# Layer 3's weights of eight steps queued on VectorE behind a block's joining

## Chip, cores and metric

The kernel runs on one core of one Trainium2 chip. The metric is the device time of one execution in microseconds (us); several executions are taken and their median is given. Beside them one execution was recorded by the profiler; all views of a profile in this text are of that one execution.

## The reference

Four graph layers follow one another on a matrix x of 3327 rows and 256 columns, with one adjacency matrix of 3327 x 3327 of which about one entry in a hundred is set. After each layer the input is added and the rows are normalised.

```python
x = _layernorm(x + _L0_gnn_ref(x, adj, L0_gnn_Wq, L0_gnn_Wk))
x = _layernorm(x + _L1_gnn_ref(x, adj, L1_gnn_W, L1_gnn_a))
x = _layernorm(x + _L2_gnn_ref(x, adj, L2_gnn_Wq, L2_gnn_bq, ...))
x = _layernorm(x + _L3_gnn_ref(x, adj, L3_gnn_W0, L3_gnn_W1, ...))
```

The change touches the last one, which is three graph attention layers behind one product with `W0`:

```python
def _gat_layer(h, adj, W, a):
    Wh = h @ W
    f1 = Wh @ a[:F_out]
    f2 = Wh @ a[F_out:]
    e = jax.nn.leaky_relu(f1 + f2.T, ALPHA)
    att = jnp.where(adj > 0, e, NEG_INF)
    att = jax.nn.softmax(att, axis=1)
    h_prime = att @ Wh
    return jax.nn.elu(h_prime)
h = input @ W0
h = _gat_layer(h, adj, W1, a1)
h = _gat_layer(h, adj, W2, a2)
h = _gat_layer(h, adj, W3, a3)
```

So each of the three makes a matrix of 3327 x 3327 weights, one for every pair of rows, sets those without an edge to nothing, multiplies the matrix with 256 columns and divides each row by its sum of weights.

## The kernel before

**Tiling and stages.** The rows are padded to 3328, 26 tiles of 128 (`NT`). The rows for which results are made are taken in 7 blocks (`NB`) of 512, the last of 256. A list of steps runs over the layers "0", "1", "2", "3a", "3b", "3c", in each over the blocks b, and in each block over the 26 tiles j of the rows that are summed over. Layer 3's three attentions are the last three entries (`deep(L)` is true for them). A loop over all steps (from L1552) traces the work of each step. All engines run at once, each through a queue of its own in a fixed order; only the first steps of the whole program have an order written out by hand. The order of the rest is found when the program is built, by a scheduler that takes what is ready by a priority and by estimated times. An edge between two instructions of one engine that carries no data binds the scheduler: the second is queued behind the first.

**Weights.** `Gat.weights` makes the weights of one step, 128 x 512: ScalarE writes `re` (L787), VectorE adds and multiplies with the mask into `ft` (L800). Blocks 0 to 5 of layer 3 use Strassen's seven products in place of eight. For these, sums and differences of quarters of the weights are needed: four instructions `qsum` for four steps together (`quad_sums`, L871 to L874), or four shorter `ssum` for two steps (L883 to L886). The other factor's sums, `tsums`, were written to memory in the layer before and are loaded again for each pair of steps, into three buffers, by SyncE's queue (L857).

`make_to(n)` (called at L1581) traces the weights of all steps below n that were not traced yet. In layer 3 it runs 7 steps ahead of the step whose products come next, so at a block's start the first weights of this block have been traced already, behind those of the block before.

**Products.** Each second step, `products` (L935) issues 14 matmuls of TensorE into four banks of PSUM, `po`. TensorE takes an fp32 matmul as two rows in the profile. 13 pairs make a block: 364 rows. PSUM has five banks for `po`.

**A block's end.** `finish` is a generator that `advance()` drives, one part behind each following step's products. It starts with `joined` (L943 to L980): it adds Strassen's products from the four banks into one tile, `p`. ScalarE copies one quarter (L961), and then 12 instructions of VectorE follow (L967 to L979); the last of them, L979, adds the last bank's part. The row sums are inverted (L1182, L1183), and then comes, for the 512 rows,

1. `normed` on ScalarE, four instructions that divide by the row sums (L1175 or L1177, in place on `p`),
2. `turn`: two copies of ScalarE that lay out the halves of the numbers as `planes` (L990), a transpose by DMA that SyncE's queue issues (L993, `turned<-planes`), and two copies by VectorE into `pT` (L1000),
3. `projected`: eight matmuls of TensorE with the next attention's W (`pproj<-w,pT`, L1230),
4. elu on ScalarE and VectorE (L1239, L1242, L1254), the scores of the next attention (L719), its sums (L1084, L844 to L852).

VectorE's queue holds, in the stretch from L967 to the copies L1000, both the joining and weights of the next steps. Which stands where is the scheduler's choice.

Of the kernel before, what the change touches and what calls it, by code (L numbers as in the profile page):

```python
# [33 lines left out]
def gnn_stack(ctx: ExitStack, tc: tile.TileContext, a: dict, N: int, out: bass.AP):  # L34
# [8 lines left out]
    nc = tc.nc  # L43
# [6 lines left out]
    def bw(b):  # L50
        return min(CH, NP - b * CH)
# [652 lines left out]
    class Gat:  # L704
        def __init__(self, key):
            self.last = key == "3c"
            self.quads = ("3a", "3b", "3c").index(key) + 1 if key != "1" else 0
            self.k = w.get("k_" + key)
            self.row = w["row_" + key]
            self.sd = cols.tile([P, 2, NT], F32, tag="sd", name="sd")  # L710
            self.th = cols.tile([P, NT], F32, tag="th", name="th")
            self.rh = cols.tile([P, NT], F32, tag="rh", name="rh")
            self.nrh = cols.tile([P, NT], F32, tag="nrh", name="nrh")
            self.u = {}
# [100 lines left out]
    def strassen(L, b):  # L815
        if L.key == "0":
            return 0 < b < NB - 1
        if deep(L):
            return b < NB - 1
        return L.key == "2"  # L820

    def deep(L):
        return L.i > 2
# [65 lines left out]
    def places(pos, b):  # L889


        o = H + 1
        m = {
            1: ((0, 0, o), (0, o, o)),
            2: ((0, 2 * o, o), (2, 0, o)),
            5: ((2, o, o), (2, 2 * o, o)),
            3: ((3, 0, H), (3, H, H)),
            4: ((3, D, H), (3, D + H, H)),
            6: ((1, 0, H), (1, H, H)),
            7: ((1, D, H), (1, D + H, H)),  # L900
        }
        return {
            k: [(g, pos[g][:, c : c + n]) for g, c, n in v[: bw(b) // D]]
            for k, v in m.items()
        }
# [37 lines left out]
    def joined(pos, b, c):  # L943

        w_ = places(pos, b)
        q = bw(b) // D
        o = H + 1

        def both(k):

            bank_, at, n = {
                1: (0, 0, o), 5: (2, o, o), 3: (3, 0, H), 4: (3, D, H), 6: (1, 0, H), 7: (1, D, H)
            }[k]
            v = pos[bank_][:, at : at + 2 * n].rearrange("p (s n) -> p s n", n=n)
            return v[:, :q, :H]

        c11, c12 = c[:, :q, H:], c[:, :q, :H]
        c21, c22 = c[:, q : 2 * q, H:], c[:, q : 2 * q, :H]
        add, sub = ALU.add, ALU.subtract
        z = cols.tile([P, 4], F32, tag="zc", name="zs")  # L960
        nc.scalar.copy(c22, both(1))  # L961

        def sums(k):
            v = pos[{1: 0, 5: 2}[k]][:, {1: 0, 5: o}[k] :]
            return v[:, : 2 * o].rearrange("p (s n) -> p s n", n=o)[:, :q, H]

        nc.vector.tensor_copy(z[:, :q], sums(1))  # L967
        nc.vector.tensor_copy(z[:, q : 2 * q], sums(5))
        for i in range(q):
            nc.vector.tensor_tensor(  # L970
                z[:, i : i + 1], z[:, i : i + 1], w_[2][i][1][:, H:], add
            )
            nc.vector.tensor_tensor(c[:, i, H:], c22[:, i], w_[2][i][1][:, :H], add)
        nc.vector.tensor_tensor(c22, c22, both(6), add)
        nc.vector.tensor_tensor(c21, c22, both(7), add)  # L975
        nc.vector.tensor_tensor(c12, c22, both(5), add)
        nc.vector.tensor_tensor(c22, c21, both(5), add)
        nc.vector.tensor_tensor(c21, c21, both(4), sub)
        nc.vector.tensor_tensor(c12, c12, both(3), add)  # L979
        return z[:, : 2 * q]  # L980


    def turn(x4, n, out, steps=3):
# [109 lines left out]
    def finish(L, b, pos):  # L1093
# [25 lines left out]
        if L.key == "0":  # L1119
            am = anyadj.pop(b)[:, :n]  # L1120

            if strassen(L, b):
                y4 = work.tile([P, 4, D], F32, tag="x4k", name="y4", bufs=2)
                z_ = joined(pos, b, y4)
                nc.vector.tensor_scalar(z_, z_, TINY, None, ALU.max)
            else:
                z_ = cols.tile([P, 4], F32, tag="zc", name="zc")
                for k in range(n):
                    nc.vector.tensor_scalar(
                        z_[:, k : k + 1], pos[k][:, D : D + 1], TINY, None, ALU.max  # L1130
                    )
# [38 lines left out]
        else:  # L1170

            def normed(out, src, r):

                if L.key in ("3b", "3c"):
                    nc.scalar.activation(out, src, AF.Identity, bias=less, scale=r)  # L1175
                else:
                    nc.scalar.mul(out, src, r)  # L1177

            p4 = work.tile([P, 4, D], F32, tag="stage", name="p4", bufs=4)
            if strassen(L, b):  # L1180
                z = joined(pos, b, p4)
                nc.vector.tensor_scalar(z, z, TINY, None, ALU.max)  # L1182
                nc.vector.reciprocal(z, z)  # L1183
                for k in range(n):
                    normed(p4[:, k, :], p4[:, k, :], z[:, k : k + 1])
            else:
                for k, t in enumerate(ts_):
                    ri = cols.tile([P, 1], F32, tag="ri", name="ri", bufs=4)
                    nc.vector.tensor_scalar(
                        ri, pos[k][:, D : D + 1], TINY, None, ALU.max  # L1190
                    )
                    nc.vector.reciprocal(ri, ri)
                    normed(p4[:, k, :], pos[k][:, :D], ri)
# [77 lines left out]
        if not L.hidden:  # L1271
# [10 lines left out]
            for k, t in enumerate(ts_):  # L1282
# [8 lines left out]
                if L.key == "3c":  # L1291
                    q = LASTP if t == NT - 1 else P
# [147 lines left out]
    class Layer:  # L1440
        def __init__(self, i, key, gat=False, hidden=False):
            self.i, self.key, self.is_gat, self.hidden = i, key, gat, hidden
            self.w = key
            self.gat = self.gat_next = self.sum = None
            self.late = []

    layers = [
        Layer(0, "0"),
# [28 lines left out]
    def make(s):  # L1477
        if s >= len(steps):
            return
        L, b, j = steps[s]  # L1480
        make_weights(L, b, j)
        if j % 2 and by_pairs(L, b, (j + 1) // 2):
            pairs[b, j + 1] = pair_weights(b, (j + 1) // 2)
            next(pairs[b, j + 1])
# [58 lines left out]
    extra = 0  # L1543
    ends = deque()

    def make_to(n):
        nonlocal upto
        while upto < n:
            make(upto)
            upto += 1  # L1550

    for s, (L, b, j) in enumerate(steps):  # L1552
# [6 lines left out]
        if j == 0:  # L1559
            wo, no = (CH, 4) if strassen(L, b) else (D + 1, len(tiles_of(b)))  # L1560
            pos = [
                ps_o.tile([P, wo], F32, tag="po", name="po") for _ in range(3 if end else no)
            ]
# [9 lines left out]
        ahead_of = s + LA + 1  # L1573
        if deep(L):
            ahead_of += 4 if b else min(4, j // 3)
            if b == 0 and pending:
                ahead_of = max(s + LA + 1, min(ahead_of, L.i * NB * NT + NT - 2))
            if not last:
                end_of = (L.i + 1) * NB * NT
                ahead_of = max(s + LA + 1, min(ahead_of, end_of))  # L1580
        make_to(ahead_of + extra)  # L1581
        if first:
            if j < 2:
                next(q1)
# [114 lines left out]
        if j == NT - 1:  # L1699
            if b == 0 and not last:  # L1700
                nl = layers[L.i + 1]
                L.sum = Sum()
                if nl.is_gat:
                    if nl.key == "1":
                        while "row_1" not in w:
                            next(setup)
                    nl.gat = Gat(nl.key)
                    L.gat_next = nl.gat
            if end:
                pending.append(finish_last(pos[1:], xm, 1))  # L1710
            else:
                pending.append(finish(L, b, pos))
            advance()
# [65 lines left out]
```

## Time and profile before

| | us |
|---|---|
| three runs | 2303.7, 2296.58, 2299.3 |
| median | 2299.3 |
| the profiled execution | 2297.41 |
| its span | 2295.6 |
| mean granted TensorE clock | 0.996 of full speed |
| layer 3's first block end (start of the joining) | 1419.8 |

The span runs from the first to the last instruction; the 1.8 us beside it are the start and the end of the execution. Layer 3's attention fills the last 38% of the span. Its stretches, from the windows of the trace (length, then busy time of TensorE, its weight loads, VectorE, ScalarE and GpSimd with the number of instructions, the granted clock, the share of the DMA engines, GB/s):

```
1420.00:1700.00 280.00, 272.38 (x2202) 263.25 (x2202) 261.96 (x632) 168.35 (x284) 6.14 (x13) 1.00 0.45 130
1700.00:1980.00 280.00, 272.86 (x2210) 264.27 (x2209) 260.56 (x619) 162.52 (x267) 3.38 (x14) 0.99 0.47 132
1980.00:2296.00 316.00, 299.18 (x2477) 291.65 (x2475) 293.39 (x721) 176.00 (x274) 0.10 (x1) 0.98 0.45 129
```

A line of a timeline has the start, the duration, the engine, the line of the kernel, the operation, output and input tiles and shapes, how many equal ones follow each other, and in brackets the idle time of the engine before it and what ended it. A line of the list of waits has who waited for whom, the time in all, how many times, and the longest. An instruction of VectorE can start up to about 0.1 us before the one ahead of it has ended, so costs in a row of instructions are read from start to start. PE is TensorE, PEld its weight loads, DVE is VectorE, ACT ScalarE, POOL GpSimd, SP SyncE.

### The profile page before, as it was taken

How to read it: one execution, taken by the hardware profiler on the slowest of the kernel's cores; microseconds unless marked ns; L12 is line 12 of the kernel's file. 1: busy time of each engine (PE TensorE's matmuls, PEld its weight loads, DVE VectorE, ACT ScalarE, POOL GpSimd, SP SyncE). 2: the span in 40 equal slices, each digit the busy share in tenths (PEclk: the TensorE clock that was granted, in tenths of full speed). 3: DMA queues.
4: the chain of work that ended last, by engine and by line, in shares of the span. 5: the costliest groups of instructions: out<-in, count | busy, mean ns of one | idle time of the engine just before them, and what ended most of it. 6: DMA issues, size and time to landing. Idle time of an engine off the chain costs nothing. (4 is left out here: it accounts for less than half of the span.)

```text
span 2295.6 us, 41529 instructions
## 1 busy us (share of the span) xinstructions
PE 2257.2 (98%) x15183; PEld 2004.7 (87%) x15183; DVE 1998.3 (87%) x5437; ACT 1210.3 (53%) x1982; POOL 49.4 (2%) x196
## 2 busy tenths in 40 slices
PE   9999999999999999999999999999999999999997
PEld 7788888888888877888888899999999999999997
DVE  7789999866777777898898889999899999899996
ACT  4667777764555423223223246555666555655653
POOL 0000001000000000000000000000000000000000
PEclk9999999999999999999999999999999999999999
DMA  8655565523222322132132254444444445355542
GB/s 281 192 178 179 186 195 187 161 84 89 78 72 55 105 61 81 56 100 81 56 99 71 74 171 130 133 136 143 124 129 137 131 134 148 98 152 169 149 122 58
DMA packets 186207, 286.13 MB, mean 125 GB/s; under 512 B 80413, under 2 KB 105492, under 8 KB 181396
## 3 DMA queue, kind: packets, MB, share of 16 engines
q1 hardware_dynamic: 185732, 283.22, 41.2%
q8 instruction: 120, 1.97, 0.4%
q14 instruction: 83, 0.68, 0.1%
q10 hardware_dynamic: 272, 0.26, 0.0%
HBM read 228.21 MB, written 38.44 MB: 116 GB/s over the span
## 5 line engine op out<-in xcount | busy, mean ns | idle before, releaser
L787 ACT ACTIVATE re<-u,nrh,th 128x512 f32<-128x512 f32 (+1 forms) x728 | 539.8, 778 | 343.0 <-DVE ft L800 179.7
L1644 PE MATMUL po<-v,e 128*128 128x257 f32 x1872 | 422.3, 381 | 0.9 <-ACT p L1177 0.8
L1644 PEld LDWEIGHTS po<-v,e 128*128 128x128 f32 x1872 | 352.6, 190 | 60.9 <-issue 9.8
L935 PE MATMUL po<-tsums,qsum 128*128 128x128 f32 (+1 forms) x2520 | 352.8, 275 | 1.4 <-DMA tsums<-t3b_d 0.7
L800 DVE SCALAR_TENSOR_TENSOR ft<-re,rh,mask 128x512 f32<-128x512 f32 x468 | 341.1, 747 | 2.6 <-ACT re L787 2.6
L935 PEld LDWEIGHTS po<-tsums,qsum 128*128 128x128 f32 x2520 | 316.2, 192 | 3.5 <-DVE qsum L873 1.6
L935 PE MATMUL po<-tsums,ssum 128*128 128x128 f32 (+1 forms) x2082 | 293.2, 276 | 4.0 <-DMA tsums<-t3a_d 1.7
L935 PE MATMUL po<-v,ft 128*128 128x129 f32 x1872 | 286.1, 276 | 1.3 <-DVE p L975 0.6
L935 PEld LDWEIGHTS po<-tsums,ssum 128*128 128x128 f32 x2082 | 262.6, 192 | 7.0 <-DVE ssum L885 2.0
L935 PEld LDWEIGHTS po<-v,ft 128*128 128x128 f32 x1872 | 248.2, 192 | 4.0 <-issue 1.8
L935 PEld LDWEIGHTS po<-v,e 128*128 128x128 f32 x1196 | 172.3, 191 | 37.6 <-issue 24.9
L935 PE MATMUL po<-v,e 128*128 128x129 f32 x1196 | 185.1, 275 | 0.0
L800 DVE SCALAR_TENSOR_TENSOR e<-re,rh,mask 128x512 f32<-128x512 f32 (+1 forms) x234 | 149.1, 657 | 38.4 <-PE po L1644 28.4
L524 ACT ACTIVATE ex<-ps,rq 128x512 f32<-128x512 f32 (+1 forms) x183 | 118.9, 652 | 114.7 <-PE ps L511 109.9
L511 PE MATMUL ps<-ft 128*128 128x512 f32 (+1 forms) x364 | 166.9, 564 | 0.0
L496 DVE SCALAR_TENSOR_TENSOR e<-ex,mask 128x512 f32<-128x512 f32 (+1 forms) x182 | 115.8, 650 | 49.0 <-ACT ex L694 27.1
L935 PE MATMUL po<-tsums,ft 128*128 128x128 f32 x936 | 144.2, 275 | 0.0
L525 DVE SCALAR_TENSOR_TENSOR e<-ex,mask 128x512 f32<-128x512 f32 (+1 forms) x183 | 116.8, 644 | 31.1 <-ACT ex L524 30.5
L686 PE MATMUL ps<-gT,ft 128*128 128x512 f32 (+1 forms) x336 | 129.8, 527 | 0.0
L935 PE MATMUL po<-v,qsum 128*128 128x128 f32 x840 | 128.8, 275 | 0.0
L935 PEld LDWEIGHTS po<-tsums,ft 128*128 128x128 f32 x936 | 124.9, 193 | 0.3
L660 ACT ACTIVATE ex<-ex,off 128x512 f32<-128x512 f32 x98 | 67.0, 716 | 101.7 <-DVE ex L676 69.1
(346 smaller groups left out, 3572.8 us busy)
## 6 DMA issues: line engine op xcount, KB each, us to landing
mask<-mask_d SPq DMA_DIRECT2D x30, 1664.0 KB
stage<-in_adj_a SPq DMA_DIRECT2D x78, 512.0 KB
tsums<-t_d SPq DMA_DIRECT2D x152, 256.5 KB
tsums<-t3a_d SPq DMA_DIRECT2D x77, 256.5 KB
tsums<-t3b_d SPq DMA_DIRECT2D x77, 256.5 KB
tsums<-t3c_d SPq DMA_DIRECT2D x77, 256.5 KB
mask_d<-mask SPq DMA_DIRECT2D x6, 1664.0 KB
u<-s_d SPq DMA_DIRECT2D x24, 256.0 KB
```

What stands on the lines that cost most here:

```text
L496: nc.vector.scalar_tensor_tensor(e[:, :wd], t_[:, :wd], 0.0, mask(b, j), ALU.add, ALU.mult)
L511: nc.tensor.matmul(ps[:, :wd], FT[j // 4][:, 0, (j % 4) * P : (j % 4 + 1) * P], FT[b][:, 1, :wd], start=True, stop=True,)
L524: nc.scalar.activation(t_[:, c], ps[:, c], AF.Exp, scale=rq[:, j : j + 1])
L525: nc.vector.scalar_tensor_tensor(e[:, c], t_[:, c], 0.0, mask(b, j)[:, c], ALU.add, ALU.mult)
L660: nc.scalar.activation(x[k], x[k], AF.Exp, bias=off, scale=1.0 / D**0.5)
L686: nc.tensor.matmul(ps[:, :wd], FT[j // 4][:, h, (j % 4) * P : (j % 4 + 1) * P], g[:, h, :wd], start=(h == 0), stop=(h == 1),)
L787: nc.scalar.activation(t_[:, :wd], self.u[b][:, :wd], AF.Relu, bias=self.nrh[:, j : j + 1], scale=self.th[:, j : j + 1],)
L800: nc.vector.scalar_tensor_tensor(e[:, :wd], t_[:, :wd], self.rh[:, j : j + 1], mask(b, j), ALU.add, ALU.mult,)
L935: nc.tensor.matmul(o, x, y, start=(p == 0 and g not in banks[:i]), stop=(p == NT // 2 - 1 and g not in banks[i + 1 :]),)
L1644: nc.tensor.matmul(pos[k], e[:, k * P : (k + 1) * P], V[L.i % 2][i], start=(i == 0), stop=(i == NT - 1),)
```

## The change

`joined` returns its last instruction (L979) too. For layer 3's blocks it is kept in the layer's `joined`, which is empty until the first block's end. In the first eight steps of each block for which there is one, `make_to` runs inside `issue_after`: each VectorE instruction that is traced in it gets an edge without data to the kept L979, so it is queued behind it. What is computed, the tiles and the other engines' instructions stay as they are; the scheduler orders all engines anew with the edges. The edges exist for blocks 1 to 6 of each of the three attentions, 18 block ends. `extra`, `LA` and the steps ahead are the same.

```diff
@@ joined @@
-        nc.vector.tensor_tensor(c12, c12, both(3), add)
-        return z[:, : 2 * q]
+        return z[:, : 2 * q], nc.vector.tensor_tensor(c12, c12, both(3), add)
@@ finish, layer "0" @@
-                z_ = joined(pos, b, y4)
+                z_, _ = joined(pos, b, y4)
@@ finish, other layers @@
-                z = joined(pos, b, p4)
+                z, L.joined = joined(pos, b, p4)
@@ class Layer @@
             self.late = []
+            self.joined = None
@@ the loop over the steps @@
-        make_to(ahead_of + extra)
+        if deep(L) and L.joined is not None and j < 8:
+            with tc.issue_after(L.joined.ins):
+                make_to(ahead_of + extra)
+        else:
+            make_to(ahead_of + extra)
```

## Prediction

> **What bounds the kernel now.** First the page's busy times and its chain, to see which engine sets the end:
>
> ```profile
> PE 2257.2 (98%) x15183; PEld 2004.7 (87%) x15183; DVE 1998.3 (87%) x5437; ACT 1210.3 (53%) x1982; POOL 49.4 (2%) x196
> ...
> PE 9%; DVE 4%; DMA 2%; ACT 1%; issue 1%; POOL 0%; DVEq 0%; ACTq 0%; POOLq 0%
> PE po L935 7%; DMA turned<-planes 1%; PE pproj L1230 1%; DVE ft L800 1%; ACT planes L990 1%; PE po L1644 1%; PE po L1610 0%; DVE v L800 0%; ACT re L787 0%; ACT p L1175 0%; DMA tsums<-t3c_d 0%; DVE qsum L872 0%; DVE qsum L874 0%; DVE pT L1000 0%; DVE qsum L873 0%
> ```
>
> TensorE is busy all the time and VectorE nearly. The chain runs through `turned<-planes`, `planes` and `pproj`, the path behind a block's end. So the question is what TensorE waits for, in the list of its waits and then where VectorE stands meanwhile:
>
> ```profile
> PE pproj L1230 <- DVE pT L1000: 13.3, 14, 2.3
> PE po L935 <- DMA tsums<-t3a_d: 1.7, 2, 1.4
> ...
> PE po L935 <- DVE p L975: 0.6, 2, 0.3
> ```
>
> The copies of the turned rows are by far the largest thing that TensorE waits for; 12.7 of the 13.3 us lie behind 1420 us, in layer 3, which alone the change touches. Next, VectorE's timeline at the block end of 1767 us (3b; columns: start, us, instruction):
>
> ```profile
> 1767.23 0.16 DVE L967 COPY zs<-po 128x2 f32<-128x2 f32 x1
> 1767.30 0.75 DVE L800 SCALAR_TENSOR_TENSOR ft<-re,rh,mask 128x512 f32<-128x512 f32 x1
> ...
> 1768.62 0.75 DVE L800 SCALAR_TENSOR_TENSOR ft<-re,rh,mask 128x512 f32<-128x512 f32 x1
> ...
> 1769.70 0.67 DVE L871 TENSOR_TENSOR qsum<-ft 128x512 f32<-128x512 f32 x1
> ...
> 1770.94 0.69 DVE L872 TENSOR_TENSOR qsum<-ft 128x512 f32<-128x512 f32 x1
> ...
> 1771.87 0.69 DVE L873 TENSOR_TENSOR qsum<-qsum,ft 128x512 f32<-128x512 f32 x1
> ...
> 1772.80 0.42 DVE L979 TENSOR_TENSOR p<-p,po 128x256 f32<-128x256 f32 x1
> 1773.13 0.69 DVE L874 TENSOR_TENSOR qsum<-ft,qsum 128x512 f32<-128x512 f32 x1
> ```
>
> Five weight instructions stand between the joining's first (L967) and last (L979). Behind it, on ScalarE four `normed` (2.08 us) and two `planes` (1.97 us), then SyncE's transpose, then the copy. At the end of 1812 us the same path, as VectorE's and TensorE's timelines show it:
>
> ```profile
> 1826.77 0.69 DVE L872 TENSOR_TENSOR qsum<-ft 128x512 f32<-128x512 f32 x1
> 1829.84 1.37 DVE L1000 COPY pT<-turned 128x1024 uint16<-128x1024 uint16 x2 [2.38 <-issue]
> ```
> ```profile
> 1831.27 4.54 PE L1230 MATMUL pproj<-w_l_w,pT 128*128 128x256 f32 x12 [2.23 <-DVE pT L1000]
> ```
>
> VectorE stands 2.38 us at the copy, TensorE 2.23 us for the copy. The transpose is late, so the path sets both engines; neither is at its own bound here. The granted clock in the windows behind this gap and the like one at 1879 us (last columns: clock, DMA share, GB/s):
>
> ```profile
> 1831.40:1834.90 3.50, 3.50 (x9) 2.79 (x10) 3.28 (x6) 1.36 (x3) 0.00 (x0) 0.51 0.00 0
> ...
> 1879.20:1882.70 3.50, 3.19 (x8) 2.57 (x9) 2.48 (x6) 1.08 (x3) 0.00 (x0) 0.51 0.00 0
> ```
>
> **The change, part by part.** Nothing is removed or added: returning L979's instruction and keeping it in `L.joined` issues nothing, and the edge is an order within VectorE's queue. So the instruction counts and the work stay, and the cost of the edit is in what moves. It acts at 18 block ends (3 sublayers, blocks 1 to 6); the other layers keep their order.
>
> *What leaves the joining.* One `ft` costs 0.66 us from start to start (1767.30 to 1767.96), one `qsum` 0.60 us (1770.94 to 1771.54). Two and three make 2 x 0.66 + 3 x 0.60 = 3.1 us at this end; two and two make 2.5 us in 3a; where six stand there, some 3.8 us. The queues of the changed program say the same: at 17 of the 18 ends these four to six stand right behind L979, and between L979 and the copy there are 14 or 15 VectorE instructions as before.
>
> *What comes earlier.* L979, `normed`, `planes` and the transpose come 2.5 to 3.8 us earlier. The transpose is now issued ahead of one `tsums` load that it followed. SyncE's timeline before:
>
> ```profile
> 1777.96 2.99 SPq L993 DMA_TRANSPOSE turned<-planes  x1
> 1781.05 0.53 SPq L857 DMA_DIRECT2D tsums<-t3b_d  x1
> ```
>
> The transpose's row is 2.99 us and the load starts at 1781.05, behind it. Now the transpose can start at about 1774.9 (behind the previous load of 1774.46), and be through at 1777.9; so the load, too, goes earlier. Cost nil; if the cover were gone, it is the 1.4 us of the worst wait for `tsums`.
>
> *What it brings to TensorE.* Its `pproj` stands 2 to 10 matmuls earlier in its queue (two rows of 0.112 us each: 0.4 to 2.2 us), and the copy comes 2.5 to 3.9 us earlier. The margin is 0.5 to 1.8 us, so the gaps should close. The gaps ahead of the first `pproj`, end by end from the trace: 3a 0.93, 0.39, 2.09, 1.72, 0, 0.48 = 5.6 us; 3b 0.02, 0.23, 2.23, 2.30, 0.66, 0.42 = 5.9 us; 3c 0, 0.41, 0.29, 0.55, 0.03 = 1.3 us, and 0.97 at the last end, where the queue moves the other way (10 matmuls later) and which I put at nothing. Two stretches of half clock of 3.4 us cost 1.7 us each and hang on the gaps of 2.23 and 2.30 us; the gap of 2.09 us at 1529 brought none.
>
> [...]
>
> *What VectorE allows.* From 1784 to 1832 us it is busy 45.5 of 48.0 us; its idle time is the 2.38 us at the copy. So a block can shrink by about this much, not by TensorE's 2.23 + 1.7. I take for those two ends VectorE's idle, 2.4 and 2.6 us: 3b then gives 0.25 + 5.0 + 1.1 = 6.3 us.
>
> *What comes later.* The moved weights come 0.7 to 2.1 us later. Queued behind them on VectorE is the weight work of the next steps, and TensorE's products wait for that. Measured from a weight's end on VectorE to its first use on TensorE, the lead at the ends is 0.7 to 1.8 us in 3a, 1.9 to 2.4 us at the first ends of 3b and 3c, 3 to 10 us after. Placed in the new order, all leads stay above 0.7 us, as the whole joining, 5.1 to 6.3 us with its guests, ends earlier by what they take. At the starts of 3b and 3c (1676 and 1982 us) the new order brings some weights, with 0.05 us of lead, 0.7 to 1.3 us later; twice nothing to 1.3 us, of which I take 0.6 each, as TensorE makes up part behind it.
>
> *Not in the trace: the transpose's landing at its new place.* It lands 4.4 us after its issue at 13 ends and 6.1 us at five (1429, 1521, 1568, 1823, 1871). At these five, 15 of its 16 semaphore steps come at 4.4 us and the last at 6.1, with a 16 KB fetch of TensorE's instructions on the queue "instruction" starting about 4.0 us after the issue. In 3c that fetch comes 5.6 to 7 us after it, and none lands late. Moved 3 us forward against TensorE's stream, the five should look like those of 3c; I take 4.4 us. If the 1.7 us stayed, 0.2 to 1.2 us of gap would be left at each, about 4 us in all.
>
> **Sum:** 5.6 + 6.3 + 1.3 - 1.2 = 12.0 us. The profiled execution took 2297.4 us (span 2295.6); 2297.4 - 12.0 = 2285.4. It lies 1.9 us under the median of 2299.3, so the forecast is 2287. Bounds of the same mechanism: all gaps, the half clock and the 0.6 us for `p`, 5.6 + 5.9 + 3.4 + 1.3 + 1.0 + 0.6 = 17.8 us, 2281; with the late landings and 2 us lost at the starts, 12 - 4 - 1.4 = 6.6 us, 2293.
>
> **The rivals.** *VectorE becomes the bound.* The gap at the copy closes, and the same time reappears as waits for `ft` and `qsum`. For it: in the middle of 3a's blocks leads are 0.05 to 0.8 us, so TensorE already goes at VectorE's pace there; per block VectorE has 44.3 to 45.5 us of work against 44.3 us of TensorE's (364 x 0.112 + 16 x 0.2175 + 0.3). Against: VectorE's only idle time in a block is that at the copy, so work that fills it is not lost. If only the two widest ends of 3b gave anything (5.0 us) and 3a's starts lost 1, the gain is 4 us: 2295.
>
> *Later weights starve TensorE (the other side).* Place: the six ends of 3a and the first of 3b and 3c, where leads are 0.7 to 2.4 us. A weight 2.1 us later at a lead of 0.7 us is a wait of 1.4 us; eight of them 11.2 us, and 3a's 5.6 us is not won. Against the 7.6 us of 3b and 3c this is +3.6 us. It passes the bound of a visible loss at (6.9 + 7.6) / 8 = 1.8 us per end. That takes the half clock as well: a wait of 1.4 us that joins a gap for the copy makes one of over 2.2 us, and four such stretches of 1.7 us bring +10.4 us: 2310. For it, the row of L800 in the chain, 1%; against it, that the weights between L979 and the copy are no more than before.
>
> *It does not do what it says*: the transpose could be held by SyncE's loads rather than by the joining. The 460 us that this queue waited for `po` speaks for it. Against: at 1777.96 it started 0.4 us behind the end of `planes` (1777.59). Its result would be that of the first rival, and it is counted there.
>
> **How the numbers follow.** Forecast 0.64, VectorE the bound or the path held elsewhere 0.23, starved 0.13. About 0.3% (6.9 us) is what a measurement of this kernel can tell from no change: faster is below 2292.4, slower above 2306.2. The forecast lies in the first, the second case within, the third above: 0.64, 0.23, 0.13. The likeliest case alone has 2281 to 2293. The range for 8 in 10 goes from 2278, under the full bound by the spread of the runs (3 us), to 2304, over the first rival and up to where the starved case begins.
>
> **What would show it.** Right: no `ft` or `qsum` between L967 and L979 in layer 3's ends; L979 to L967 in some 2.5 us; "PE pproj <- DVE pT" falls from 13.3 to under 3 us; no half clock at about 1831 and 1879; landings of 4.4 us at all ends. Wrong: waits of "PE po <- DVE ft" or "qsum" of several us in 3a, or VectorE's idle time at the copy as before. The forecast fails above all if TensorE's idle time moves from `pproj` to `po`, with the busy sums of a block unchanged.

## The result and the profile after

The changed kernel takes 2285.99 us (median of 6 runs, 2284.7 to 2286.95), the kernel before 2297.71 us (median of 6, the three of the table above among them, 2296.58 to 2303.7). The ratio is 0.9944, 95% interval 0.9931 to 0.9957: faster by 0.56%. The profiled execution has a span of 2283.0 us; before it was 2295.6.

The page of the changed kernel, busy times and chain:

```profile
PE 2251.7 (99%) x15183; PEld 2001.1 (88%) x15183; DVE 2001.4 (88%) x5437; ACT 1206.6 (53%) x1982; POOL 45.8 (2%) x196
...
PE 5%; DVE 4%; ACT 1%; DMA 1%; issue 1%; SPq 0%; DVEq 0%; ACTq 0%
```

The instructions are the same in number and VectorE's busy time is the same within 0.2%; what went is waiting. (Behind L979 every line has a number one lower than before: the copy is L999, `pproj` is L1229.) TensorE's list of waits in the changed kernel:

```profile
PE pproj L1229 <- DVE pT L999: 6.1, 14, 1.0
PE po L935 <- DVE qsum L873: 1.5, 3, 0.7
PE po L935 <- DMA tsums<-t3b_d: 1.5, 3, 0.6
PE po L935 <- DVE ft L800: 1.3, 3, 0.8
```

The wait for the copies fell from 13.3 to 6.1 us and its longest from 2.3 to 1.0 us. VectorE's timeline at 3b's third block end, the one that stood at 1812 us:

```profile
1804.94 0.14 DVE L967 COPY zs<-po 128x2 f32<-128x2 f32 x1
...
1806.15 0.16 DVE L968 COPY zs<-po 128x2 f32<-128x2 f32 x1 [0.68 <-PE po L935]
...
1808.71 0.41 DVE L979 TENSOR_TENSOR p<-p,po 128x256 f32<-128x256 f32 x1
1809.04 1.41 DVE L800 SCALAR_TENSOR_TENSOR ft<-re,rh,mask 128x512 f32<-128x512 f32 x2
...
1818.16 0.75 DVE L999 COPY pT<-turned 128x1024 uint16<-128x1024 uint16 x1 [0.19 <-issue]
```
```profile
1820.19 2.86 PE L1229 MATMUL pproj<-w_l_w,pT 128*128 128x256 f32 x12 [0.23 <-DVE pT L999]
```

No weight stands between L967 and L979 any more. The joining takes 4.2 us and not 5.9, though it now waits 0.68 us for the last bank of TensorE. The copy follows 9.0 us behind the joining's end (before 11.4) and TensorE waits 0.23 us and not 2.23.

Where the time went, by sublayer. The windows are cut at the same matmuls of TensorE's list in both kernels (6900, 4800, 2450 and 150 rows ahead of its last). First the kernel before, then the changed one (window, length, busy time of TensorE, its weight loads, VectorE, ScalarE, GpSimd, then clock, DMA share, GB/s):

```profile
1418.20:1685.90 267.70, 260.09 (x2103) 251.38 (x2102) 249.66 (x605) 161.52 (x270) 6.14 (x13) 1.00 0.47 135
1685.90:1985.50 299.60, 291.76 (x2353) 282.10 (x2352) 278.56 (x663) 176.20 (x291) 3.38 (x14) 0.99 0.46 132
1985.50:2260.50 275.00, 273.02 (x2303) 267.83 (x2302) 272.52 (x641) 167.22 (x255) 0.10 (x1) 1.00 0.48 138
```
```profile
1417.90:1679.10 261.20, 259.09 (x2102) 251.25 (x2101) 251.79 (x607) 160.24 (x271) 2.76 (x13) 1.00 0.48 138
1679.10:1972.00 292.90, 287.60 (x2352) 279.53 (x2351) 279.02 (x661) 174.46 (x290) 4.47 (x14) 1.00 0.47 135
1972.00:2247.70 275.70, 272.75 (x2302) 267.62 (x2301) 271.02 (x628) 165.32 (x254) 0.10 (x1) 1.00 0.48 137
```

3a is shorter by 6.5 us, 3b by 6.7 us, 3c longer by 0.7 us; with 0.3 us ahead of it and -0.2 us behind, that makes the 12.6 us of the spans. In 3b, 4.2 us of TensorE's busy time went too, 3.4 us of it the two stretches of half clock.

So far this is the forecast, 2287 us. But one thing that the prediction had put as a side condition changed too, and leaves the reason open: the five late landings were gone as well. In the kernel before, the transposes of the ends at 1419, 1511, 1558, 1812 and 1860 us landed 6.0 to 6.5 us after their issue, which is where its five gaps of 0.9 to 2.3 us are; in the changed kernel all land within 4.8 us. DMA packets by queue, in the 4.5 us from the transpose's issue; first the kernel before (issue 1823.45), then the changed one (issue 1813.51):

```profile
q1 hardware_dynamic: 2238, 0.82, 87.9%
q8 instruction: 1, 0.02, 1.3%
```
```profile
q1 hardware_dynamic: 2268, 0.88, 94.8%
```

Before, one 16 KB packet of the queue "instruction" falls into the transpose; after, none does. Either the shorter path closed the gaps or the moved fetch did, and the experiments had to part the two.

### The profile page after: what moved, and what is told of

It reads as the page before. It is cut to its first block, busy times and chain, and to the rows that moved or that the text cites. A ratio compares the mean times of both kernels' runs of the same rounds, so it can differ in the third digit from the quotient of the medians.

```text
span 2283.0 us, 41500 instructions
## 1 busy us (share of the span) xinstructions
PE 2251.7 (99%) x15183; PEld 2001.1 (88%) x15183; DVE 2001.4 (88%) x5437; ACT 1206.6 (53%) x1982; POOL 45.8 (2%) x196
```

## The experiments

Three explanations were put against each other. Theory P is the prediction's: the joining without weights makes the path shorter, and this closes the gaps. Rivals at first: only the clock (the half-clock stretches), and a better order of all engines by chance. From the fifth run on the rival is theory F: a fetch of TensorE's instructions that falls into a transpose delays its last part, and the change moved the transposes away from the fetches.

**One sublayer at a time (e1, e2, e3).** The edit (against the changed kernel), for 3a; 3b and 3c alike:

```diff
-        if deep(L) and L.joined is not None and j < 8:
+        if L.key == "3a" and L.joined is not None and j < 8:
```

> The edges act in 3a alone. Theory (the joining without weights brings the whole path behind it forward, and each gap ahead of pproj closes): 3a's gaps of 5.6 us close and 3b and 3c keep theirs, so about 2297.7 - 6 = 2291.7 us, joinings of some 3.4 us in 3a and of 5 to 6.6 us after; gap of TensorE ahead of the first pproj about 0 at 3a's first five ends and still over 2 us at two ends of 3b. Rival 1 (only the clock: what was won is the half-clock stretches): nothing of the 5.6 us shows, 2297 us, as 3a had no half clock at its ends. Rival 2 (a better order of all engines by chance): no sum from the single parts to the whole can be foretold.

> The edges act in 3b alone. Theory: gaps of 5.9 us plus up to two half-clock stretches of 1.7 us, limited by VectorE's idle time to some 6.3 us, so 2291.5 us; 3a's gaps of 5.6 us stay. Rival 1 (only the clock): 3.4 us, 2294.3 us. Rival 2 (order by chance): not foretold.

> The edges act in 3c alone. Theory: gaps of 1.3 us are there to close; the trace of the changed kernel shows 3c 0.7 us longer than before, as SyncE's loads and pproj's earlier place take it back, so 2297.7 + 0.5 us, within 2 us of before. Rival 1 (only the clock): 2297.7. Rival 2 (order by chance): a gain of some us is as likely as a loss.

Measured: 3a alone 2292.57 us, ratio 0.9975 (0.9965 to 0.9985); 3b alone 2292.25 us, 0.9973 (0.9962 to 0.9984); 3c alone 2296.62 us, 0.9996 (0.9986 to 1.0005). The kernel before took 2298.6 us beside them. So 3a gives 6.0 us, 3b 6.4 us, 3c 2.0 us at most or nothing, as P has it, and the sum 12.4 to 14.4 us stands beside the 11.7 us of the whole. "Only the clock" falls: 3a has no half clock at its ends. But these runs can't part P from F, since each sublayer's edges also took its late landings away: 3a alone has none in 3a and four in 3b; 3b alone none in 3b and three in 3a.

**The edges for two steps only (e4).** The order of the whole program changes, but the weights stay in the joinings.

```diff
-        if deep(L) and L.joined is not None and j < 8:
+        if deep(L) and L.joined is not None and j < 2:
```

> All three sublayers, but only the weights traced in a block's first two steps get the edge: the whole program is ordered anew, yet at 15 of the 18 ends four or five weight instructions still stand in the joining. Theory: the gaps ahead of pproj stay at these ends, 2297.7 - 1 = 2296.7 us, at most 3 us from before. Rival 2 (the gain is another order of TensorE, ScalarE and SyncE, not what stands in the joining): most of the 11.7 us is there, 2286 to 2290 us. Rival 1 (only the clock): anything between 2292 and 2298, by whether half-clock stretches appear.

Measured 2286.45 us, ratio 0.9949 (0.9936 to 0.9961): the whole gain, with joinings of 5.6 to 6.9 us that hold four or five weight instructions at 15 of the 18 ends. P failed here by 10 us; the rival "a better order by chance" had 2286 to 2290 us, and these runs do not exclude it. What this kernel does share with the changed one is few late landings: three, in place of five. Where its landings are on time, `pproj` waits 0 to 0.1 us at the regular ends, although the path is as long as before: the copy starts 12.7 to 16.0 us behind the block's last product there, before 13.7 to 17.1. So a path of the old length leaves no gap in this order, if the landing is on time.

**The fetches moved, nothing else (e5, e6, e7, e8).** The fetches are the packets of 16 KB on q8, "instruction": 120 in the kernel before, one for about every 127 of TensorE's 15183 rows. Matmuls more or fewer at the very start should therefore shift all later fetches against the work, while every engine's order in layer 3 stays as it was.

```diff
-    for _ in range(8):
+    for _ in range(0):
         nc.tensor.matmul(turned[:, :P], ones, ones, start=True, stop=True)
```

This edit was made to the kernel before (e5), to the changed kernel (e7) and to the kernel of e4 (e8); the changed kernel with `range(26)` is e6. As the orders stay, "a better order" forecasts no change for e5 and e6, like P.

> The kernel before with the 8 matmuls at its very start left out (their result is overwritten unread); all engines' orders in layer 3 stay as before. The 16 KB fetches of TensorE's instructions then fall 8 matmuls, some 1.8 us, later against the work: at 5.6 us or more behind each transpose's issue instead of 3.8 to 4.5. Theory F (a fetch that starts 3.8 to 4.5 us behind a transpose's issue delays the transpose's last part by 1.6 us, and that made the wide gaps): no landing of 6 us in layer 3, the five gaps of 0.9 to 2.3 us fall to 0 to 0.6, no half clock at 1831 and 1879: from 1420 us on 9 to 11 us shorter than before, with unchanged joinings of 5.5 to 6.6 us. Theory P (the joining without weights, a path 2.5 us shorter, is what closes them): nothing changes in layer 3. The start may cost up to 2 us, as the first matmuls are then the ones at half clock.

> The changed kernel with 18 more matmuls at its start (26 instead of 8, result overwritten unread), orders in layer 3 as in the changed kernel. The fetches fall some 4 us earlier: in 3b and 3c from 7.4 to 8.2 us behind a transpose's issue to 3.4 to 4.2, in 3a from 5 to 6.4 to 1 to 2.4. Theory F: landings of about 6 us at most of the ten ends of 3b and 3c, gaps ahead of pproj of 1.5 to 2.2 us there although the joinings hold no weights, some with a half clock: 15 to 20 us longer from 1700 us on. Theory P: layer 3 as in the changed kernel, within 2 us. Either way 4 us more at the start.

> The changed kernel without the 8 matmuls at its start: the control of the other three. Its fetches move from 5 to 8.2 us behind the transposes to 7 to 10, still clear of them. Both theories: layer 3 as in the changed kernel, 2286 us, and up to 2 us more or less from the start alone.

> The kernel with edges for a block's first two steps (four or five weights still in most joinings), without the 8 matmuls at its start. Theory F: its three landings of 6 us (3b's and 3c's first ends and 3c's second) go, with gaps of 1.7, 1.7 and 2.1 us and a half clock of 1.7 us: 7 us under the 2286.5 us it took, 2279.5 plus what the start costs. Theory P: the same 2286.5 plus the start.

Measured, beside 2297.78 us of the kernel before: e5 2288.99 us, ratio 0.9961 (0.9949 to 0.9973); e6 2315.21 us, 1.0082 (1.0068 to 1.0095); e7 2288.11 us, 0.9959 (0.9947 to 0.997); e8 2282.39 us, 0.9934 (0.9922 to 0.9945).

F holds in both directions. The kernel before, with its joinings and its orders in layer 3 as they were, wins 8.8 us when its fetches come later (9 to 11 had been expected; the 4.5 us behind the transpose of the end below, issued at 1818.94, hold no packet of "instruction" any more); and the changed kernel, with joinings free of weights, becomes slower than the kernel before when its fetches come earlier. VectorE's and TensorE's lines in e5 at the end where before they waited 2.38 and 2.23 us:

```profile
1823.48 1.37 DVE L1000 COPY pT<-turned 128x1024 uint16<-128x1024 uint16 x2 [0.54 <-issue]
```
```profile
1824.90 2.86 PE L1230 MATMUL pproj<-w_l_w,pT 128*128 128x256 f32 x12 [0.38 <-DVE pT L1000]
```

And e6 at an end of 3c, where SyncE issued the transpose at 2181.83; its packets in the 4.5 us from then, VectorE's copy, TensorE's `pproj`, and TensorE's waits for the copies in all:

```profile
q1 hardware_dynamic: 2221, 0.80, 100.9%
q8 instruction: 1, 0.02, 1.6%
```
```profile
2177.01 0.41 DVE L979 TENSOR_TENSOR p<-p,po 128x256 f32<-128x256 f32 x1
2188.42 0.74 DVE L999 COPY pT<-turned 128x1024 uint16<-128x1024 uint16 x1 [2.15 <-DMA turned<-planes]
```
```profile
2190.44 2.86 PE L1229 MATMUL pproj<-w_l_w,pT 128*128 128x256 f32 x12 [2.17 <-DVE pT L999]
```
```profile
PE pproj L1229 <- DVE pT L999: 22.5, 19, 2.2
```

The fetch is in the transpose again, the copy comes 6.6 us after the issue, and the gap that the change should have closed is there, at a joining without a single weight. The landing is late at 14 of the 18 ends, and at 12 of them the gap is 1.0 to 2.2 us. Of the 29 us by which e6 is slower than the changed kernel, 19 lie in 3b and 3c (15 to 20 had been expected), 6 in 3a, for which no loss had been named, and some 5 ahead of layer 3.

e7 is the control: with the start alike, the changed kernel (e7) is 0.9 us under the kernel before (e5; 2288.11 against 2288.99), and the two intervals lie on each other. e7 is 2.1 us over the changed kernel with its own start. By the traces (spans of 2286.0 and 2283.0 us) 1.2 us of the difference lie ahead of layer 3 and 1.8 in 3c, with no late landing in either kernel; the reason is open.

e8 went the way of F, but only in part: 4.1 us under e4, where up to 7 had been expected.

**The same by sublayer.** From the traces of all kernels but one (one execution each), the time of each sublayer in us (between the same matmuls as above) and the late landings in it; a landing counts as late where the copy waits for it and starts over 5.2 us after the transpose's issue:

| kernel | 3a | late | 3b | late | 3c | late |
|---|---|---|---|---|---|---|
| before | 267.7 | 3 | 299.6 | 2 | 275.0 | 0 |
| changed | 261.2 | 0 | 292.9 | 0 | 275.7 | 0 |
| e1, edges in 3a | 261.3 | 0 | 301.4 | 4 | 275.3 | 0 |
| e2, edges in 3b | 267.3 | 3 | 291.7 | 0 | 277.1 | 0 |
| e3, edges in 3c | 267.2 | 3 | 300.7 | 3 | 275.1 | 0 |
| e4, two steps | 261.6 | 0 | 292.9 | 1 | 280.0 | 2 |
| e5, before, fetch later | 262.4 | 0 | 294.8 | 0 | 276.5 | 0 |
| e6, changed, fetch earlier | 267.0 | 5 | 303.6 | 5 | 284.0 | 4 |
| e7, changed, fetch later | 261.2 | 0 | 292.9 | 0 | 277.5 | 0 |
| e8, two steps, fetch later | 261.0 | 0 | 291.0 | 0 | 274.2 | 0 |
| e10, before, fetch a bit later (below) | 263.4 | 0 | 294.2 | 0 | 276.1 | 0 |

Read down a column: the time follows the late landings far more than the edges. Without late landings 3a takes 261.0 to 263.4 us, 3b 291.0 to 294.8 us, 3c 274.2 to 277.5 us, with weights in the joining or without.

**The fetch later by half as much (e10).** The kernel before with `range(4)`.

> The kernel before with 4 instead of 8 matmuls at its start, so that the fetches fall 0.9 us later and not 1.8. Theory F: the landings of 6 us in 3a (fetches at 4.0 to 4.5 us, not held back) go, as the fetch then starts behind the last part at 4.9 or more; those of 3b, where the fetch is held until 4 us, may stay: two to three landings fewer, 2292 us, between before and e5 (2289.0). Theory P: 2297.7 as before.

Measured 2290.76 us beside 2297.51, ratio 0.9971 (0.9961 to 0.9982): between, as expected. No landing is late, which is more than was expected, but five fetches still start 4.0 to 4.3 us behind an issue; that a fetch is held in 3b, as had been assumed, was not shown. A fetch there is thus not always harmful, and it was not in the kernel before: at four more of its ends, 1466, 1722, 1767 and 1909 us, the fetch starts 4.0 to 4.2 us behind the issue and the landing is on time. Over the 198 block ends of eleven kernels (both that are compared and all of the study but e9, whose copies are queued behind other work): where the fetch starts up to 5.0 us behind the issue, 35 of 62 landings are late; from 5.0 us on, 0 of 92; without a fetch near, 0 of 44.

**The gaps that are left (e9).** With the fetches out of the way the changed kernel still waits 0.3 to 0.7 us for `pT` at 3b's and 3c's ends (1.0 at the last). In the new order `pproj` stands 58 matmuls behind its block's last product and not 66 to 69: the scheduler moved it forward with the path.

```diff
-        return (9 if L.key == "3c" else 7) if b == NB - 2 else 4
+        return (9 if L.key == "3c" else 7) if b == NB - 2 else 6 if deep(L) else 4
```

> The changed kernel with the fetches later (no matmuls at the start, as the control e7) and one number changed: the turn of layer 3's blocks takes six steps and not four, which puts the first pproj 61 to 65 matmuls behind its block's last product in 3b and 3c and not 58 (before: 66 to 69). Theory: the 3 us shorter path gave almost nothing because pproj was queued 9 matmuls earlier with it; with 3 to 7 matmuls (0.7 to 1.6 us) more, the gaps of 0.3 to 0.6 us at 3b's and 3c's ends (6.3 us in all in the control) fall to under 2 us: 2288.1 - 4 = 2284 us. Rival: VectorE is the bound, the gaps close and come back as waits for weights: 2288 us.

Measured 2284.65 us, ratio 0.9945 (0.9932 to 0.9959), 3.5 us under the control e7. The two were measured at different times, with the kernel before at 2297.51 and 2297.78 us; their intervals overlap, but no run of e9 (2283.62 to 2286.31) is as slow as one of e7 (2287.31 to 2289.24). TensorE's waits for the copies in e9:

```profile
PE pproj L1229 <- DVE pT L999: 3.3, 8, 0.9
```

At layer 3's ends they are 2.6 us in all, against 6.3 in e7 (under 2 had been expected). The gaps closed and the time came off: VectorE was not the bound yet. By sublayer of one execution each, 3c won 3.7 us and 3b 1.3, while 3a, where e7 had no gaps but at its last end, lost 1.5.

e8 (edges for two steps, fetches later) is the fastest kernel of the study: 2282.39 us, 3.6 us under the changed kernel by the medians. Most of its joinings hold weights, and no fetch falls into a transpose. Against e5, which has the same start and no late landing either, it wins 6.6 us: the gaps ahead of the first `pproj` are 2.3 us in all there and 5.6 in e5. So the order that a scheduler finds is worth some us beside the fetches, and the joining without weights is not what gives it; no run here parts what does.

## Why the prediction was right, and where its reason was not

The time, 2287 us against 2285.99, was right, and so was the sign. The sum priced gaps that close, and they closed; that they did so for the other reason, as the transposes came to lie clear of the fetches at all 18 ends, is in part luck. By its own steps:

- *What leaves the joining* and *what comes earlier*: right. No weight is left in it, the joinings take 3.3 to 5.0 us (before 4.3 to 6.7), and the copy starts 10.5 to 13.7 us behind the block's last product (before 11.4 to 17.1). The 3.1 us at an end with five weights were not all won: at 3b's and 3c's ends VectorE now waits for the last bank, as in the line of 1806.15.
- *"The margin is 0.5 to 1.8 us, so the gaps should close"*: this is the step that failed, as a cause. The sum by sublayer came out (3a 5.6 forecast, 6.5 measured; 3b 6.3 and 6.7), but e5 shows 5.3 us of 3a's and 4.8 us of 3b's with nothing moved ahead of the transpose, and e6 shows gaps of 1.0 to 2.2 us at twelve ends, at the shorter path. At ends with a landing on time there was little to close (0 to 0.7 us), and there the shorter path was taken back: `pproj` moved forward by 8 to 10 matmuls, 1.8 to 2.2 us, and 0.2 to 0.5 us of gap stayed.
- *"I take 4.4 us" for the late landings*: the choice was right, as was the sign of it, a fetch moved out of the transpose. Its price was not: it was booked as a condition worth "about 4 us in all", with 12 us on the path's account. It also overlooked that besides the five late ends four with the landing on time had the fetch at 4.0 to 4.2 us. The fetch alone is worth 8.8 us (e5), and what the edges add where no fetch is in the way is 0.9 us by e7 against e5, and 3.0 us if the changed kernel's own start is kept (2285.99 against 2288.99). Which of the two it is stays open; the difference lies ahead of layer 3 and in 3c, as said for e7.
- *Half clock*: right. Both stretches went with their gaps, 3.4 us (clock 1.00 in the changed kernel's three windows).
- *3c, 1.3 us forecast*: wrong in sign by the traces, 0.7 us longer (one execution each; 3c alone, e3, gave 2.0 us at most or nothing). Its gaps before were as small as those that the change leaves.
- *The transpose ahead of one load of `tsums`, cost nil*: nearly. TensorE's waits for `tsums` of 3b went from 0.9 to 1.5 us.
- *What VectorE allows* and the rival that VectorE becomes the bound: it did not, as e8 and e9 go lower still. (TensorE's 44.3 us a block come to 44.5 by the terms given; nothing hangs on it.) *Starved TensorE*: waits for `ft` and `qsum` are 1.3 and 1.5 us in all in the changed kernel; the leads were read rightly. *That it does not do what it says*: it does, but that is not what pays.

## What to carry to other kernels

A wait that ends with a DMA has a landing to be explained before the work ahead of it is: ask why the same transfer takes 4.4 us at one place and 6.1 at another. In this long unrolled program the fetches of TensorE's instructions ran by DMA beside its transfers, one of 16 KB for about 127 rows, and 8 matmuls fewer at its start were enough for no transpose of layer 3 to land late (e5; 5 of 18 before). So an edit that changes counts or order can win or lose by moving a fetch into or out of a critical transfer, here 0.4% (e5) and 1.3% (e6 against the changed kernel). Shift the fetches alone, as a control, before the gain is put down to the edit.

## What the runs showed of the hardware

**A fetch in a transpose.** In the eleven kernels counted above, a transpose that lands on time has its last of 16 semaphore steps 4.2 to 5.1 us from its issue. The 35 late ones are of two kinds. In 27 the transpose's packets of 256 bytes are through as usual and 14 or 15 of the steps come by 5.1 us, the last at 5.9 to 6.6. At the five late ends of the kernel before the 16th step comes 1.5 to 1.9 us behind the 15th, and the copy starts 0.03 to 0.12 us behind the 16th (4.48, 6.01 and 6.04 us from the issue of 1429.40). In the other eight, all in e6, these packets cease for 0.3 to 0.9 us behind the fetch's start, and all 16 steps come late, at 5.1 to 6.3 us. The queue in e6, behind the transpose issued at 1877.91 whose fetch starts 2.2 us after it, in the windows 1879.91:1880.41 and 1880.91:1881.41 (packets, MB, share of 16 engines):

```profile
q1 hardware_dynamic: 395, 0.10, 182.4%
```
```profile
q1 hardware_dynamic: 13, 0.00, 6.5%
```

In all five transposes in which 460 or more of the 2048 packets were still to come when the fetch started, all 16 steps were late. With 85 or fewer to come, the whole transpose was late three times, the last step alone 27 times, and 27 times nothing was. In the kernel before, TensorE's 15183 rows, each with its weight load, have 120 fetches of 16 KB. No wait in TensorE's list is for one; what they cost shows at the transposes, 8.8 us (2297.78 against 2288.99 us in e5). How a fetch delays a transpose was not shown, as the traces do not name a packet's DMA engine; nor why 27 of the 62 near fetches did no harm.

**Half clock behind some gaps.** In the kernel before a stretch lasts 3.413 us at a clock of 0.50. Its gaps of 2.23 and 2.30 us ahead of `pproj` were each followed by one, those of 2.09 and 1.72 us (1529 and 1576 us) by none. A wait of only 1.38 us for `tsums`, up to 1379.9 us, was followed by one too, from 1380.9 to 1384.3 us. In e1 gaps of 2.35 us brought no half clock, in e4 one of 2.08 us brought one. So the size of the gap alone does not tell. In e6 the stretches begin at 1742.8, 1790.6 and 1838.4 us, 47.8 us apart, as do those of the kernel before (1831.4 and 1879.2): 14 times the 3.413 us that one lasts; from 1380.9 to 1831.4 us it is 132 times. What decides whether a gap brings a stretch was not shown.
